# Attention and FP4 feed-forward on one core: two periods as one pattern, later due times, and a last block by tiles on VectorE

## The chip, the core and the metric

The kernel runs on one core of a Trainium2 chip. Times are device microseconds of one execution; the kernel before took 3674.7 us (median of 3 runs, 3671.81 to 3677.18). A profile is one further execution. Engines in its rows: PE is TensorE's matmuls, PEld its weight loads, DVE is VectorE, ACT ScalarE, POOL GpSimd, SP the engine that issues most transfers. PSUM is the accumulator memory that TensorE writes; a tile of 128 x 512 f32 fills one of its 8 banks.

## What is computed

One transformer block on x of 4 x 2048 x 256, f32: attention with 16 heads of 16, a layer norm, a gated feed-forward whose inputs and weights are quantized to FP4 in blocks of 16, and a second norm.

```python
q, k, v = (split_heads(x @ W.T) for W in (Wq, Wk, Wv))        # 16 heads of 16
attn = softmax(q @ k.T * 0.25)
x = layernorm(x + merge(attn @ v) @ Wo.T)

def fp4_linear(x, w):       # both through fp4_quant_dequant: per block of 16,
    ...                     # scale = max|x| / 6, x / scale to the nearest of
    ...                     # 0 .5 1 1.5 2 3 4 6, times scale
h = silu(fp4_linear(x, w_gate)) * fp4_linear(x, w_up)         # 704 columns
x = layernorm(x + fp4_linear(h, w_down))
```

## The kernel before

**Steps and periods.** A step is one batch entry, one block of 512 queries (QB) and one group of four heads: 64 steps. Each goes over 16 tiles of 128 keys; one key tile of one step is a *period*, so there are N = 1024. In period n three things happen for the attention. `maxima` (L394) forms scores for the step that is LEAD = 20 periods ahead: two calls (i = 0, 1), each two matmuls `pm`, of the heads j = 0 and 1 of a pair, into one tile of two banks, from which VectorE takes a maximum per row (`mx`, L409). `exponentials` (L435) forms the scores transposed, four matmuls `pe`, each into a bank of its own, and ScalarE takes the exponential of each into an `e` tile (L443). `values` (L446) multiplies the four `e` tiles of LAG = 2 periods ago with v, into the one bank `av`.

The score matmuls use half of the array's 128 rows: head j = 0 lies in rows 0 to 63 (the upper half below), j = 1 in rows 64 to 127 (the lower half). The row maxima are folded into two spare rows of q (`max_rows`, L411), so that the exponential needs no bias. At a step's end `normalize` (L460) copies `av` out, turns it (`pa`), and VectorE divides (`rd`, `oq`); every second step `oq` is turned (`pr`) into `oT`.

**Parts.** All other work of TensorE is cut into parts by generators: projections of q, k and v (`project`: `ptx`, `pq`, `pv`), the weights' preparation (`prepare`), and per query block `feed_forward` (L597): residual `py`, transposes `ptq`, gates `pg` and `pu`, transposes `pth`, and `pz`. A part ends at a `yield` of its cost; costs of LEAST = 300 and more count. `period` (L666) takes one counted part from the urgent queue (`max_rows`, `normalize`) or the queue, at the end of each period, two in the 20 periods before the first exponentials.

**Order.** TensorE runs in program order as written (`keep_in_program_order`, L133). In each period it is pm of i = 0 and 1, pe of i = 0, av, pe of i = 1, then the part. The other engines' orders are made by the framework's scheduler from the dependences. The 8 banks: `ps_m` two tiles of two banks (pm), `ps_av` one, `ps_x` three in turn for every pe and every part. `later` (L116) puts a step on a list by a due period: the quantization (`fp4`, L145) is so split, since its first half goes from VectorE (block maximum `amax`, scale `sc`, reciprocal `rs`) to GpSimd (`xn`), and its second (`rounded`) from VectorE (`m`) to GpSimd (three steps on `xn`, L163 to L165). GpSimd also does residual adds, gate products and the norm.

**Loads.** q, k and v go to DRAM once (`qx`, `kx`, `vx`; v through two tiles `vt`) and are loaded per step: k a quarter at a time in every fourth period, 28 periods ahead of its exponentials and 8 ahead of its maxima, into 20 tiles of `k`.

**The end.** After the last period the queue runs on alone. The last query block, whose feed-forward can begin only then, takes VectorE instead of GpSimd for every second tile.

Of the kernel before, what the change touches and what calls it, by code (L numbers as in the profile page):

```python
# [29 lines left out]
F32 = mybir.dt.float32  # L32
F32R = mybir.dt.float32r
I32 = mybir.dt.int32
# [18 lines left out]
LEAD = 20  # L53
LAG = 2
LEAST = 300.0
PSUM = bass.MemoryType.PSUM
# [17 lines left out]
def block_kernel(  # L74
# [69 lines left out]

    def fp4(pool, t, tag, gain=1.0, engine=None):  # L145

        p, nb, _ = t.shape
        amax = pool.tile([p, nb], F32, tag="amax" + tag, name="amax")
        nc.vector.tensor_reduce(amax, t, AX.X, ALU.max, apply_absolute_value=True)  # L149
        sc = pool.tile([p, nb], F32, tag="sc" + tag, name="sc")  # L150
        nc.vector.tensor_scalar(sc, amax, gain / 6.0, 1e-12, ALU.mult, ALU.max)
        rs = pool.tile([p, nb], F32, tag="rs" + tag, name="rs")
        nc.vector.reciprocal(rs, sc)
        engine = engine or nc.gpsimd
        engine.tensor_scalar(rs, rs, gain * TIES_DOWN, 1.0, ALU.mult, ALU.mult)
        xn = pool.tile([p, nb, FB], F32, tag="xn" + tag, name="xn", bufs=3 if tag else 2)
        engine.tensor_tensor(xn, t, rs.unsqueeze(2).to_broadcast([p, nb, FB]), ALU.mult)

        def rounded():
            m = pool.tile([p, nb, FB], F32, tag="m" + tag, name="m", bufs=1)  # L160
            nc.vector.tensor_single_scalar(m.bitcast(I32), xn.bitcast(I32), EXPONENT, ALU.bitwise_and)
            nc.vector.tensor_scalar(m, m, 1.0, ROUND, ALU.max, ALU.mult)  # L162
            engine.tensor_tensor(xn, xn, m, ALU.add)  # L163
            engine.tensor_tensor(xn, xn, m, ALU.subtract)  # L164
            engine.tensor_tensor(xn, xn, sc.unsqueeze(2).to_broadcast([p, nb, FB]), ALU.mult)  # L165

        return xn, later(1, rounded, 4 if tag == "" else 2)

# [12 lines left out]
    wdT = const.tile([P, NFC, D], F32, tag="wdT", name="wdT")  # L181
    vt = [const.tile([P, NG, QT // 2, NP, 3 * DH], F32, tag=f"vt{i}", name=f"vt{i}") for i in range(2)]
    for t in vt:
# [60 lines left out]
    def prepare():  # L244
# [9 lines left out]
        nc.scalar.copy(woT.rearrange("p k n -> p (k n)"), pt)  # L254
        yield 500

# [36 lines left out]
        for piece, after in zip(pieces, pieces[1:] + [None]):  # L293
            following = load(*after) if after else None
            yield from transposed(*piece, *q)
            q = following
            yield 500

# [13 lines left out]
    def project(b, tb, what):  # L312
# [7 lines left out]
        for kc in range(KC):  # L320
            pt = psum("ptx")
            for t in range(QT):
                transpose(pt[:, t * P : (t + 1) * P], xb[:, t, kc * P : (kc + 1) * P], ident)
            nc.scalar.copy(xT[:, kc, :], pt)
            yield 600
        for name, c in [(w[0], int(w[1])) for w in what if w != "v"]:
            w, dst = (wkT, kx[b % 2][c][:, :, rows]) if name == "k" else (wqT, qx[(b * NQB + tb) % len(qx)][c])
# [16 lines left out]
            projected.add((b, tb, name + str(c)))  # L344
        for t in range(QT if "v" in what else 0):
            v = vt[t // 2]
            pv = psum("pv")
            for kc in range(KC):
                matmul(
                    pv[:, :D], xT[:, kc, t * P : (t + 1) * P], wvT[:, kc, :], start=(kc == 0), stop=(kc == KC - 1)  # L350
                )
            src = pv[:, :D].rearrange("p (g i j d) -> p g i j d", g=NG, i=NP, j=2)
            for j in range(2):
                nc.scalar.copy(v[:, :, t % 2, :, 2 * j * DH : (2 * j + 1) * DH], src[:, :, :, j, :])
            if t % 2:
                t0 = tb * QT + t - 1
                for g in range(NG):
                    nc.sync.dma_start(vx[b % 2][g, :, t0 : t0 + 2, :], v[:, g].rearrange("p t i c -> p t (i c)"))
            if t == QT - 1:
                projected.add((b, tb, "v"))  # L360
            yield 900

# [14 lines left out]
    def load_k(s, kb):  # L377
        b, qb, g = steps[s]
        for i in range(NP):
            c, h = divmod(g * HG + i * 2, NC)  # L380
            k = p1.tile([P, QB], F32R, tag="k", name="k", bufs=20)
            for j in range(2):
                nc.sync.dma_start(
                    k[R * j : R * j + R, :].bitcast(F32), kx[b % 2][c][:, h + j, kb * QB : (kb + 1) * QB]
                )
            k_sb[s, i, kb] = k
# [47 lines left out]

    def exponentials(s, kt, i):  # L435
        kb, col = kt // QT, kt % QT * P
        pe = [psum("pe") for _ in range(2)]
        for j in range(2):
            rows = slice(R * j, R * j + R)
            matmul(pe[j], k_sb[s, i, kb][rows, col : col + P], q_sb[s, i][rows, :], start=True, stop=True)  # L440
        for j in range(2):
            e = p1.tile([P, QB], F32, tag="e", name="e", bufs=10)
            nc.scalar.activation(e, pe[j], AF.Exp, scale=SCALE)  # L443
            e_sb[s, kt, 2 * i + j] = e

# [14 lines left out]
    def normalize(s):  # L460
# [15 lines left out]
        for i in range(NP):  # L476
# [5 lines left out]
            )  # L482
        yield 500
        if s % 2 == 0:
            return
        yield 0
        pr = psum("pr")
# [4 lines left out]
        oTs[s // 2] = oT  # L492
        yield 500

# [18 lines left out]
    def residual(b, qb, x1, xq):  # L513

        for t in range(QT):
# [10 lines left out]
            if t % 2:  # L526
                layer_norm(x1, t - 1, 2)
                tiles = x1[:, t - 1 : t + 1].rearrange("p t (b f) -> p (t b) f", f=FB)
                later(3, lambda tiles=tiles: xq.append(fp4(p2, tiles, "")))
            yield 900  # L530

    def gated(xqT, h, t, engine):
        for half in range(2):
# [14 lines left out]
            nc.scalar.activation(a, pg[:, :FH], AF.Tanh, scale=0.5)  # L548
            engine.tensor_mul(a, a, g)  # L549
            engine.tensor_add(a, a, g)  # L550
            yield 1200
# [10 lines left out]
            nc.scalar.copy(u, pu[:, :FH])  # L562
            engine.tensor_mul(h[:, cols], a, u)  # L563
            yield 1200

    def turned(hq, tiles, hT):
# [4 lines left out]
        for t in range(2):  # L571
# [3 lines left out]
            nc.scalar.copy(hT[:, t, :4, :].rearrange("p c n -> p (c n)"), pt)  # L575
            yield 500
        pt = psum("pth").rearrange("p (t c n) -> p t c n", t=2, c=2)
# [4 lines left out]
        for c in range(4, NFC):  # L582
            w = min(P, FF - c * P)
            nc.scalar.copy(hT[:w, :, c, :], pt[:w, :, c - 4, :])
        yield 500

# [10 lines left out]
    def feed_forward(b, qb, between):  # L597
        rows = slice(qb * QB, (qb + 1) * QB)
        last = b == B - 1 and qb == NQB - 1
        x1 = p1.tile([P, QT, D], F32, tag="x1", name="x1", bufs=2)  # L600
# [11 lines left out]
        for kc in range(KC):  # L612
# [4 lines left out]
            nc.scalar.copy(xqT[:, kc, :], pt)  # L617
            yield 500
        hq = {}

        def gate(t):

            engine = nc.vector if last and t % 2 else nc.gpsimd
            h = p2.tile([P, FF], F32, tag="h", name="h")
            yield from gated(xqT, h, t, engine)
            blocks = h.rearrange("p (b f) -> p b f", f=FB)
            later(1, lambda: hq.update({t: fp4(p2, blocks, "h", gain=0.5, engine=engine)}))

        def out_rows(t):
            layer_norm(x1, t, 2)  # L630
            at = slice(qb * QB + t * P, qb * QB + (t + 2) * P)
            nc.sync.dma_start(out[b, at, :].rearrange("(t p) d -> p t d", p=P), x1[:, t : t + 2, :])

# [17 lines left out]
        out_rows(2)  # L651


    queue, urgent = deque(), deque()
# [10 lines left out]

    def period(parts):  # L666

        take_due()
        for _ in range(len(urgent)):
# [5 lines left out]
        while parts > 0 and queue:  # L675
            parts -= (part(queue) or 0.0) >= LEAST

# [28 lines left out]

    for n in range(-LEAD, N + LAG):
        m = n + LEAD
        (sm, im), (s, kt), (sv, kv) = divmod(m, NKT), divmod(n, NKT), divmod(n - LAG, NKT)
        if m in (8, 10, 12, 14):  # L710
# [17 lines left out]

        for i in range(NP):
            if m < N:  # L730
                maxima(sm, im, i)
        for i in range(NP):
            if 0 <= n < N:
                exponentials(s, kt, i)
            if i == 0 and n >= LAG:
                values(sv, kv)
        if m < N and im == NKT - 1:
            urgent.append(max_rows(sm))
        if n >= LAG and kv == NKT - 1:
            urgent.append(normalize(sv))  # L740
            if sv % NG == NG - 1:
                queue.append(chain(*steps[sv][:2]))
        period(1 if n >= 0 else 2)
    banks["more"] = True
    while urgent or queue or due:
        period(1)

# [32 lines left out]
```

## Time and profile before

| what | where it is read | value |
|---|---|---|
| median of the runs | times | 3674.7 us |
| the profiled execution, its own time | times | 3676.19 us |
| its span, first to last instruction | page | 3674.4 us |
| first av, and first pm of period 20 | timeline | 106.17, 97.3 us |
| last pm; end of attention | timeline | 3516.7, 3581.2 us |
| mx: reductions on VectorE | groups | 2048 of 1217 ns, 2409.1 us |
| e: exponentials on ScalarE | groups | 4096 of 596 ns, 2217.9 us |
| transfers, mean | page | 89 GB/s |

The page gives busy time per engine, the chain of work that ended last, and the costliest groups. A period's length is read from the timeline as the distance between two first pm matmuls. By the kind of part that stands in a period, the trace has these means over all of the loop: pg 3.78 us (120 periods), pu 3.78 (120), pq 3.54 (110), pv 3.39 (48), py 3.43 (60), pth 3.06 (73), pa 3.07 (59), pn 3.05 (48), and 2.73 where there is none (104, the median 2.61). TensorE's clock was granted in full from 300 to 3581 us but for 3.4 us, 0.91 to 0.92 before and 0.75 after.

### The profile page before, as it was taken

The page shows a single profiled execution, that of the slowest core. Times are in us where ns is not written, and L with a number is a line of the kernel's source. Part 1 is how long each engine was busy: PE and PEld are TensorE (multiplying, and loading weights), DVE is VectorE, ACT ScalarE, POOL GpSimd, SP SyncE. Part 2 cuts the span into 40 slices and gives each one's busy share as a digit, 9 for nine tenths or more (in the row PEclk, how much of TensorE's full clock was granted, in tenths as well). Part 3 has the DMA queues.
Part 4 walks back from the last instruction along what each step waited for, and adds up shares of the span by engine and source line. Part 5 has one row for each costly group of instructions (what it writes and reads, how often), then busy time and mean ns, then how long its engine had stood idle before and what let it go on. Part 6 is the DMA issues. An engine that isn't in the chain of part 4 may idle for free.

```text
span 3674.4 us, 57830 instructions
## 1 busy us (share of the span) xinstructions
PE 3535.7 (96%) x21396; PEld 1598.0 (43%) x21396; DVE 2805.1 (76%) x3250; ACT 2692.1 (73%) x5452; POOL 1292.8 (35%) x1542
## 2 busy tenths in 40 slices
PE   7889999999999999999999999999999999999995
PEld 4333444444444444444444444444443434444343
DVE  4777878777787878778787787877778788878824
ACT  3667777777777777777777777777777777777772
POOL 1340423424243242424324253343424325241525
PEclk9999999999999999999999999999999999999997
DMA  6543323323232322323233232332322222222100
GB/s 207 176 128 100 106 75 106 99 75 111 80 95 91 106 82 84 115 68 115 84 91 100 85 101 79 100 92 70 115 79 59 75 81 59 73 68 87 47 7 6
DMA packets 192146, 328.41 MB, mean 89 GB/s; under 512 B 25848, under 2 KB 69752, under 8 KB 191864
## 3 DMA queue, kind: packets, MB, share of 16 engines
q1 hardware_dynamic: 190472, 323.39, 28.7%
q8 instruction: 171, 2.80, 0.3%
q10 hardware_dynamic: 1392, 1.31, 0.1%
q14 instruction: 111, 0.91, 0.1%
HBM read 237.04 MB, written 86.51 MB: 88 GB/s over the span
## 4 chain that ended last, share of the span: by engine, by line
PE 82%; DVE 12%; POOL 3%; DMA 2%; ACT 1%; issue 1%; SPq 0%; POOLq 0%; ACTq 0%; DVEq 0%
PE av L134 24%; PE pe L134 18%; PE pm L134 15%; DVE mx L409 8%; PE pz L134 6%; PE pg L134 5%; PE pu L134 5%; PE pq L134 3%; PE pv L134 2%; PE pth L137 1%; DMA q<-qx 1%; PE pa L137 1%; PE py L134 1%; PE pn L137 1%; DVE amax L149 1%; DVE st L501 1%
## 5 line engine op out<-in xcount | busy, mean ns | idle before, releaser
L409 DVE TENSOR_REDUCE mx<-pm 128x2 f32<-128x1024 f32 x2048 | 2409.1, 1217 | 670.2 <-PE pm L134 665.7
L443 ACT ACTIVATE e<-pe 128x512 f32<-128x512 f32 x4096 | 2217.9, 596 | 678.4 <-PE pe L134 672.7
L134 PE MATMUL av<-e,v 128*32 128x512 f32 x8192 | 1097.1, 607 | 1.4 <-DMA v<-vx 1.4
L134 PE MATMUL pe<-q,k 64*128 64x512 f32 x4096 | 1035.4, 456 | 5.0 <-ACT e L443 4.7
L134 PEld LDWEIGHTS pe<-q,k 64*128 64x128 f32 x4096 | 475.1, 184 | 967.3 <-ACT e L443 853.4
L134 PE MATMUL pm<-k,q 62*128 62x512 f32 x4096 | 804.4, 448 | 69.2 <-DVE mx L409 59.6
L134 PEld LDWEIGHTS pm<-k,q 62*128 62x128 f32 x4096 | 346.5, 185 | 384.2 <-DVE mx L409 177.4
L134 PEld LDWEIGHTS av<-e,v 128*32 128x32 f32 x8192 | 162.1, 108 | 333.1 <-issue 313.2
L549 POOL TENSOR_TENSOR a<-a,g 128x352 f32<-128x352 f32 x124 | 116.1, 936 | 499.6 <-ACT a L548 499.6
L594 POOL TENSOR_TENSOR x<-x,read 128x128 f32<-128x128 f32 x128 | 59.0, 461 | 494.2 <-ACT read L142 494.2
L134 PE MATMUL pz<-wdT,hT 128*128 128x128 f32 (+1 forms) x1536 | 231.2, 293 | 0.0
L163 POOL TENSOR_TENSOR xn<-xn,m 128x704 f32<-128x704 f32 (+2 forms) x104 | 159.6, 1534 | 154.6 <-DVE m L162 136.0
L134 PEld LDWEIGHTS pz<-wdT,hT 128*128 128x128 f32 (+1 forms) x1536 | 191.9, 191 | 45.8 <-ACT e L443 18.2
L563 POOL TENSOR_TENSOR h<-a,u 128x352 f32<-128x352 f32 x124 | 116.1, 937 | 227.0 <-ACT u L562 224.6
L525 POOL TENSOR_TENSOR x<-x,read 128x256 f32<-128x256 f32 x64 | 46.7, 730 | 400.4 <-ACT read L142 400.2
L134 PE MATMUL pg<-wgT,xqT 128*128 128x352 f32 x512 | 187.0, 488 | 0.0
L134 PE MATMUL pu<-wuT,xqT 128*128 128x352 f32 x512 | 185.2, 484 | 0.0
L164 POOL TENSOR_TENSOR xn<-xn,m 128x704 f32<-128x704 f32 (+2 forms) x104 | 159.9, 1538 | 5.7
L165 POOL TENSOR_TENSOR xn<-xn,sc 128x704 f32<-128x704 f32 (+2 forms) x104 | 131.5, 1264 | 7.8
L550 POOL TENSOR_TENSOR a<-a,g 128x352 f32<-128x352 f32 x124 | 118.9, 958 | 9.7
L134 PEld LDWEIGHTS pg<-wgT,xqT 128*128 128x128 f32 x512 | 88.2, 191 | 58.4 <-ACT e L443 19.2
L134 PEld LDWEIGHTS pu<-wuT,xqT 128*128 128x128 f32 x512 | 87.7, 189 | 58.4 <-ACT e L443 20.0
(95 smaller groups left out, 2277.3 us busy)
## 6 DMA issues: line engine op xcount, KB each, us to landing
k<-kx SPq DMA_DIRECT2D x1024, 128.0 KB
v<-vx SPq DMA_DIRECT2D x64, 768.0 KB
q<-qx SPq DMA_DIRECT2D x256, 124.0 KB
kx<-khi SPq DMA_DIRECT2D x64, 256.0 KB
qx<-qhi SPq DMA_DIRECT2D x64, 256.0 KB
vx<-vt SPq DMA_DIRECT2D x128, 96.0 KB
xb<-in_L_attn_x_dram SPq DMA_DIRECT2D x16, 512.0 KB
kx<-klo SPq DMA_DIRECT2D x32, 256.0 KB
```

The source lines that it names most:

```text
L134: tc.keep_in_program_order(nc.tensor.matmul(*args, **kw))
L137: tc.keep_in_program_order(nc.tensor.transpose(*args))
L163: engine.tensor_tensor(xn, xn, m, ALU.add)
L164: engine.tensor_tensor(xn, xn, m, ALU.subtract)
L165: engine.tensor_tensor(xn, xn, sc.unsqueeze(2).to_broadcast([p, nb, FB]), ALU.mult)
L409: nc.vector.tensor_reduce(mx_sb[s][:, t, 2 * i : 2 * i + 2, kb], pm, AX.X, ALU.max)
L443: nc.scalar.activation(e, pe[j], AF.Exp, scale=SCALE)
L525: nc.gpsimd.tensor_add(x1[:, t, :], x1[:, t, :], read(py[:, :D]))
L549: engine.tensor_mul(a, a, g)
L550: engine.tensor_add(a, a, g)
L563: engine.tensor_mul(h[:, cols], a, u)
L594: nc.gpsimd.tensor_add(x1[:, t, cols], x1[:, t, cols], read(pz))
```

## The change

Two periods become one pattern, given by a string. In it m and n are the two `maxima` of the even and the odd period, e and f the four exponentials of each, one by one, v and w the values; q takes two parts in a row, r what q left over. `more` replaces `period`; a part whose cost is TIED ends a row of two early. `max_rows` and `normalize` are begun at once and no longer at the end of the period.

```diff
+ORDER = "m0 e0 m1 e1 q e2 n0 e3 v n1 f0 f1 r f2 w f3".split()
+TIED = 500.0
+E_BUFS = 12
...
-    def exponentials(s, kt, i):
+    def exponentials(s, kt, h):
+        i, j = divmod(h, 2)
         kb, col = kt // QT, kt % QT * P
-        pe = [psum("pe") for _ in range(2)]
-        for j in range(2):
-            rows = slice(R * j, R * j + R)
-            matmul(pe[j], k_sb[s, i, kb][rows, col : col + P], q_sb[s, i][rows, :], start=True, stop=True)
...
+        pe = psum("pe")
+        rows = slice(R * j, R * j + R)
+        matmul(pe, k_sb[s, i, kb][rows, col : col + P], q_sb[s, i][rows, :], start=True, stop=True)
+        e = p1.tile([P, QB], F32, tag="e", name="e", bufs=E_BUFS)
...
         while parts > 0 and queue:
-            parts -= (part(queue) or 0.0) >= LEAST
+            cost = part(queue) or 0.0
+            parts -= cost >= LEAST
+            if cost == TIED:
+                break
+        return parts
...
-    for n in range(-LEAD, N + LAG):
+    for n in range(-LEAD, N + LAG, 2):
+        left = 0
+        if n == N - NKT:
+            x1_last = load_last(*steps[-1][:2])
+        for step in ORDER:
+            n_of = n + (step[0] in "nfwr")
+            m = n_of + LEAD
+            if step in ("m0", "n0"):
+                loads(n_of)
+                take_due()
+            if step[0] in "mn" and m < N:
+                maxima(*divmod(m, NKT), int(step[1]))
+                if step == "n1" and (m + 1) % NKT == 0:
+                    begin(max_rows(m // NKT))
+            elif step[0] in "ef" and 0 <= n < N:
+                exponentials(*divmod(n_of, NKT), int(step[1]))
+            elif step in "vw" and n >= LAG:
+                s, kt = divmod(n_of - LAG, NKT)
+                values(s, kt)
+                if kt == NKT - 1:
+                    begin(normalize(s))
+                    if s % NG == NG - 1 and s + 1 < len(steps):
+                        queue.append(chain(*steps[s][:2]))
+            elif step == "q":
+                left = more(2)
+            elif step == "r" and n < 0:
+                more(2)
+            elif step == "r":
+                while left > 0 and queue:
+                    left -= (part(queue) or 0.0) >= LEAST
...
+    feed_forward_last(*steps[-1][:2], x1_last)
```

Buffers, the v transfers and the due times:

```diff
-            k = p1.tile([P, QB], F32R, tag="k", name="k", bufs=20)
+            k = p1.tile([P, QB], F32R, tag="k", name="k", bufs=16)
...
+                v = vt[(tb * 2 + t // 2) % 3]
...
-                for g in range(NG):
-                    nc.sync.dma_start(vx[b % 2][g, :, t0 : t0 + 2, :], v[:, g].rearrange("p t i c -> p t (i c)"))
+                    nc.sync.dma_start(
+                        vx[b % 2][:, :, t0 : t0 + 2, :].rearrange("g p t c -> p g (t c)"),
+                        v.rearrange("p g t i c -> p g (t i c)"),
+                    )
...
-        return xn, later(1, rounded, 4 if tag == "" else 2)
+        return xn, later(2, rounded, 4 if tag == "" else 2)
...
-                layer_norm(x1, t - 1, 2)
-                tiles = x1[:, t - 1 : t + 1].rearrange("p t (b f) -> p (t b) f", f=FB)
-                later(3, lambda tiles=tiles: xq.append(fp4(p2, tiles, "")))
+                def normed(t=t):
+                    layer_norm(x1, t - 1, 2)
+                    tiles = x1[:, t - 1 : t + 1].rearrange("p t (b f) -> p (t b) f", f=FB)
+                    later(4, lambda: xq.append(fp4(p2, tiles, "")))
+                later(2, normed)
...
-            later(1, lambda: hq.update({t: fp4(p2, blocks, "h", gain=0.5, engine=engine)}))
+            later(3, lambda: hq.update({t: fp4(p2, blocks, "h", gain=0.5)}))
```

The last query block has functions of its own, which go tile by tile. In them VectorE does what GpSimd did, but for two small steps of the norm (`rstd`); `fp4_at_once` is the whole of `fp4` on VectorE.

```diff
+        def moments(t):
+            st = p2.tile([P, 6], F32, tag="st", name="st")
+            nc.vector.bn_stats(st, x1[:, t, :])
...
+            nc.gpsimd.tensor_scalar_add(rstd[:, :1], mv[:, 0, 1:2], LN_EPS)
+            nc.gpsimd.tensor_tensor(rstd[:, :1], rstd[:, :1], minus_half[:, :1], ALU.pow)
...
+        def attended(t):
...
+            nc.vector.tensor_add(x1[:, t, :], x1[:, t, :], py[:, :D])
+            moments(t)
+        def quantized(t):
+            normed(t)
+            xq[t] = fp4_at_once(p2, x1[:, t].rearrange("p (b f) -> p b f", f=FB), "")
...
+        def hidden(t):
+            h = p2.tile([P, FF], F32, tag="h", name="h")
+            for half, (a, g, u) in enumerate(gates.pop(t)):
+                nc.vector.scalar_tensor_tensor(a, a, 1.0, g, ALU.add, ALU.mult)
+                nc.vector.tensor_mul(h[:, half * FH : (half + 1) * FH], a, u)
+            hq[t] = fp4_at_once(p2, h.rearrange("p (b f) -> p b f", f=FB), "h", gain=0.5)
...
+        attended(0)
+        attended(1)
+        quantized(0)
+        up(0)
+        attended(2)
+        quantized(1)
+        up(1)
+        hidden(0)
+        attended(3)
+        quantized(2)
+        pz = downward(0)
+        up(2)
+        hidden(1)
+        added(0, pz)
+        quantized(3)
+        pz = downward(1)
+        up(3)
+        hidden(2)
+        stored(0)
+        added(1, pz)
+        pz = downward(2)
+        hidden(3)
+        stored(1)
+        added(2, pz)
+        pz = downward(3)
+        stored(2)
+        added(3, pz)
+        stored(3)
```

Here `up` is a tile's transposes and its pg and pu, `downward` its pth and pz, `stored` the norm's last step and the store.

## The prediction

> **What bounds the kernel now.** I read the page's engine shares and chain of waits first, then the windows by stage, the timeline of TensorE inside two periods, the waits between 300 and 3540 us, and last the groups by form for prices.
>
> ```profile
> PE 3535.7 (96%) x21396; PEld 1598.0 (43%) x21396; DVE 2805.1 (76%) x3250; ACT 2692.1 (73%) x5452; POOL 1292.8 (35%) x1542
> PE 82%; DVE 12%; POOL 3%; DMA 2%; ACT 1%; issue 1%; SPq 0%; POOLq 0%; ACTq 0%; DVEq 0%
> ...
> 300.00:3516.70 3216.70, 3177.84 (x19481) 1413.26 (x19479) 2564.98 (x2941) 2455.60 (x4931) 1144.74 (x1356) 1.00 0.28 86
> 3516.70:3581.20 64.50, 60.16 (x375) 25.35 (x371) 7.08 (x19) 48.31 (x99) 14.27 (x23) 1.00 0.03 9
> 3581.20:3674.40 93.20, 49.42 (x216) 36.23 (x216) 40.11 (x71) 19.65 (x48) 52.97 (x64) 0.75 0.02 6
> ```
>
> TensorE is the path for 3,480 us; the last 93 us belong to GpSimd and VectorE by turns. Inside the loop, two neighbouring periods:
>
> ```profile
> 2012.09 0.73 PE L134 MATMUL pm<-k,q 62*128 62x512 f32 x4
> 2012.66 0.57 PE L134 MATMUL pe<-q,k 64*128 64x512 f32 x2
> 2013.16 1.07 PE L134 MATMUL av<-e,v 128*32 128x512 f32 x8
> 2014.16 0.50 PE L134 MATMUL pe<-q,k 64*128 64x512 f32 x2
> 2014.59 0.66 PE L137 MATMUL pth<-ident,xn 128*128 128x128 f32 x4
> 2015.17 0.73 PE L134 MATMUL pm<-k,q 62*128 62x512 f32 x4
> 2015.74 0.58 PE L134 MATMUL pe<-q,k 64*128 64x512 f32 x2
> 2016.26 1.06 PE L134 MATMUL av<-e,v 128*32 128x512 f32 x8
> 2017.25 0.49 PE L134 MATMUL pe<-q,k 64*128 64x512 f32 x2
> 2017.68 1.45 PE L134 MATMUL pg<-wgT,xqT 128*128 128x352 f32 x4
> 2019.06 0.50 PE L134 MATMUL pm<-k,q 62*128 62x512 f32 x2
> ```
>
> Read the starts. The period with pg takes 3.89 us, of which 0.19 is a wait of pe for its bank; the shortest such period of the trace is 3.70. Its pieces: pm 0.57, pe 0.33, av 1.00, pe 0.43, pg 1.38. A pair of score matmuls on the two row halves of the array costs one "unit": within pm it is 0.231 us (timeline at 2015.51 to 2015.74). Each stretch of score matmuls carries about 0.195 more, being 0.10 ahead of its second unit and 0.10 at its end, and a part carries 0.20 (pg: four passes of 0.295 make 1.18 of the 1.38). So a period with a part costs TensorE 2.32 + 0.20 + W, W being the part's passes: pg 1.18, pq, pv and py 0.86, pz 1.32, four transposes 0.40. The medians of the trace bear this out (pg 3.72, pq 3.39). From period 80 on, 942 periods took 3187.5 us, where these sums give 3044: 143 us are waits.
>
> ```profile
> PEld pe L134 <- ACT e L443: 786.7, 1029, 1.3
> ...
> PEld pm L134 <- DVE mx L409: 144.8, 363, 1.2
> ```
>
> The first line is mostly weight loads ready early; it costs only the 0.18 us of short periods (pth, 3.10 instead of 2.92). The second is the real wait, a VectorE that has not emptied pm.
>
> **The skill.** "TensorEngine Tiling (Array Packing)", Key Properties, says that a change of tiling mode drains the array and that tiles run independently; the 0.2 us per change and the paired starts agree. "TensorE: Matmul & The Clock Gate", Part 3, The mechanism, says that matmuls themselves keep strict program order. This trace differs:
>
> ```profile
> 1172.14 0.50 PE L134 MATMUL pm<-k,q 62*128 62x512 f32 x1
> 1172.35 0.27 PE L134 MATMUL pz<-wdT,hT 64*128 64x128 f32 x1
> 1172.38 0.47 PE L134 MATMUL pm<-k,q 62*128 62x512 f32 x1
> ```
>
> In the program both pz passes (upper rows) stand before both pm; yet a pm starts 0.2 us ahead of the second pz. I take it for the lower half passing what waits for the upper. "Perfetto Trace Analysis", Optimization Strategy, says that consistent bubbles can mean that PSUM has no room for the next tile; pth's 0.18 us agrees.
>
> **The change part by part.**
>
> (1) TensorE's order. Per two periods, score stretches fall from four to three, part stretches from two to one. That is -0.195 - 0.20 = -0.40 us. But the score matmuls no longer go in pairs. Counting each row half as its own stream: f3 m0 e0 m1 e1 is 4 units (lower half f3, m0, m1, e1), e2 n0 e3 is 2, n1 f0 f1 f2 is 3. Nine units for eight: +0.23. Sum: 9 x 0.231 + 3 x 0.195 + 2.0 for av = 4.67, +0.20 + W = 4.87 + W, against 5.03 + W before; -0.16. Without a part the first two stretches join: 6 + 3 units, 4.47. From the order of TensorE's instructions, the 501 double periods with both kinds of scores hold 736 us of W; 36 have no part. Base: 465 x 4.87 + 36 x 4.47 + 736 = 3162 us, for what took 3418.8 us (97.3 to 3516.2).
>
> (2) The waits that come back, walked through with durations of the trace (pe to activation 0.43, or 0.53 at a stretch's start; exponential 0.49 apart, 0.60 long; reduction 1.18; release to load 0.05 to 0.17).
> - The first part takes f3's bank: free at 0.53 + 0.60 + 0.05 = 1.18, wanted at 1.12. 465 x 0.06 = 28.
> - No part: n0 needs m0's buffer, free at 0.77 + 1.18 + 0.17 = 2.12; the double then lasts 5.67, 1.2 over its base. 36 x 1.2 = 43. Before, such periods took 2.61 each.
> - pa keeps its bank until VectorE, behind m0 and m1 (to 3.13), has done rd and oq (0.75). With a second part e3 wants it: 4.05 against 3.0 to 3.3; 38 x 0.84 = 32. Alone (23 times, oq behind n0): 1.6 each, 37. Before, pa cost no wait (mean 3.07).
> - Nine single pn or pr: 4. VectorE's other steps, 396 us in all (2805.1 - 2409.1), meet short doubles in about a hundred cases: 30 as an estimate, 0 to 100.
> - Weight preparation before period 80: some 45 of today's 54 stay.
> Sum 3162 + 219 = 3381, so -38. The large e pool, 16 instead of 20 k buffers and the later due times cost nothing while a load has eight periods (about 26 us) to land; SyncE now waits for the last exponentials of period n-1 before it issues k, and behind it stand q, v and the kx writes, which are wanted later still.
>
> (3) Start: a third vt and one vx transfer for four. ScalarE's 19.7 us of waits on vx shrink; TensorE's share of that was 4.4 us at 75.97 and four smaller ones. -8.
>
> (4) Periods without maxima: 22, now 2.93 each; the long stretches spread the exponentials, -3.
>
> (5) The last block. Today GpSimd's quantization and VectorE's share one chain:
>
> ```profile
> L164 POOL TENSOR_TENSOR xn<-xn,m 128x704 f32<-128x704 f32 x64 | 109.0, 1703 | 2.6
> L164 DVE TENSOR_TENSOR xn<-xn,m 128x704 f32<-128x704 f32 x2 | 1.8, 875 | 0.0
> ```
>
> On VectorE alone a tile costs: residual add 0.42, moments 0.59, norm 0.25, quantize 256 columns 3.0, gates 4 x 0.5, quantize 704 columns 6.3, and 0.42 + 0.59 + 0.25 at the end: 13.8, four tiles 55, some 3 less as neighbours overlap. Ahead of it stands what stands there now, 4.3 us to the first add; behind the last quantization come transposes, copies, pz, norm and store, 9 us, of which 2.6 lie under the sum. 4.3 + 52 + 4 of waits + 9 = 69, against 93.2. -24. A GpSimd that works alongside made VectorE's add 1.26 us instead of 0.88; here GpSimd has only rstd. Bounds: -30 with no waits, -10 if each tile waits 4 us for TensorE.
>
> Sum: 3674.4 - 38 - 8 - 3 - 24 = 3601 us of span; the profiled run reports 3676.2 for a span of 3674.4, and the median is 3674.7, so 3602.
>
> **The rivals.**
> A, slower: matmuls keep strict order across the halves, as the skill says. e2 n0 e3 is then 3 units, 10 in all: 465 x 0.231 = +107, 3709. It decides from 0.15 us per double on (73 / 501). Against it speaks 1172.14, for it that this is one pattern of few matmuls.
> B: the waits of VectorE's in-order queue eat the loop's gain: 70 us instead of 30, and pa more. Only start and end remain: 3640 to 3680. For it: VectorE is 76% busy and 5.5 of a double's 6.7 us.
> C: the waits in (2) hardly occur, since the chains run half a period apart: 120 us less, 3500 to 3530. For it, 143 us of waits now sit at pm, which the new order separates by whole stretches.
> That the change doesn't do what it says: the instruction order shows the alternation in all 501 doubles; only the r slot is almost never filled.
>
> **Numbers.** Main case 3565 to 3640: 0.58. A 0.15. B 0.17, of which 0.05 within 0.2% and 0.01 slower. C 0.10. A measurement here tells 0.2% (7 us) from no change. Faster 0.79, same 0.05, slower 0.16. The range 3530 to 3690 leaves out A and half of C.
>
> **What would show it.** Right: three score stretches of about 1.1, 0.66 and 0.9 us per double, n0 starting beside e2 and not after it; big doubles (pg with pu) of 7.2 to 7.4 us against 7.55; empty ones near 5.7; pa doubles long; a tail of about 70 us. Wrong: e2 n0 e3 of 0.9 us; VectorE's lag showing as waits of pm in long doubles; a tail over 85 us; or a lower granted clock in the loop, now 1.00.

## The result and the profile after

The changed kernel takes 3798.1 us (median of six runs, 3794.6 to 3799.7) against 3674.8 for the kernel before, run beside it: a ratio of 1.033, interval 1.032 to 1.035. The forecast was 3602, so even its sign was wrong. The profiled execution has a span of 3793.1 us, against 3674.4.

The engine shares and the chain of waits from the page of the changed kernel, then its windows by stage (columns: busy us and instructions of PE, PEld, DVE, ACT and POOL, granted clock, transfers):

```profile
PE 3587.7 (95%) x21348; PEld 1653.3 (44%) x21348; DVE 2821.5 (74%) x3310; ACT 2648.3 (70%) x5446; POOL 1259.7 (33%) x1495
PE 70%; DVE 16%; POOL 6%; ACT 4%; issue 3%; DMA 1%; SPq 0%; POOLq 0%; ACTq 0%; DVEq 0%
```

```profile
300.00:3646.10 3346.10, 3216.22 (x19403) 1462.12 (x19403) 2559.20 (x2928) 2407.96 (x4912) 1152.08 (x1353) 0.99 0.28 83
3646.10:3716.90 70.80, 67.48 (x406) 30.41 (x402) 8.13 (x21) 50.88 (x105) 19.86 (x29) 1.00 0.02 7
3716.90:3793.10 76.20, 49.56 (x168) 31.77 (x168) 50.64 (x131) 16.24 (x42) 8.52 (x16) 0.85 0.03 9
```

Read the chain first: TensorE's share fell from 82% to 70%, and VectorE and GpSimd together rose from 15% to 22%. The rows of the windows then say where: the long one (the loop) is 129 us longer than before, the last (the tail) 17 us shorter. TensorE was idle for 129.9 us of the loop's window; before it was 38.9. By stage, with the loop counted from the first pm of period 20 to the last pm:

| stage, us | before | forecast | after |
|---|---|---|---|
| start, to the first pm of period 20 | 97.3 | 89 | 92.8 |
| loop | 3419.4 | 3381 | 3553.4 |
| periods without maxima | 63.8 | 61 | 69.9 |
| tail, from the last av | 93.9 | 70 | 77.0 |

The waits of VectorE between 300 and 3500 us (us in total, times, longest) show what is new. Before:

```profile
DVE mx L409 <- PE pm L134: 605.2, 578, 2.3
DVE rd L472 <- PE pa L137: 13.5, 30, 0.6
DVE m L161 <- POOL xn L157: 5.1, 26, 0.2
DVE st L501 <- POOL x L525: 3.4, 15, 0.2
```

After:

```profile
DVE mx L443 <- PE pe L140: 396.8, 440, 3.9
DVE st L533 <- POOL x L630: 121.6, 56, 2.9
DVE mx L443 <- PE pm L140: 109.1, 241, 1.8
DVE amax L155 <- POOL x L541: 56.3, 28, 2.5
DVE amax L155 <- POOL h L599: 42.4, 39, 1.4
DVE m L166 <- POOL xn L162: 18.5, 25, 0.7
DVE st L533 <- POOL x L557: 6.9, 14, 0.5
```

A VectorE that waits for TensorE (mx) is only ahead of it, and that costs nothing. A VectorE that waits for GpSimd holds up everything behind in its queue, also the reductions that TensorE needs. Those waits were 8.5 us and are 245.7. TensorE's waits for them, in the same stretch of the changed kernel:

```profile
PE pm L140 <- DVE mx L443: 96.1, 127, 4.4
...
PEld pm L140 <- DVE mx L443: 274.5, 288, 4.7
...
PEld pm L140 <- DVE st L533: 44.3, 52, 1.5
```

Before, the first two were 37.6 and 144.8, and the third was 5.0. One such place, as the timelines of VectorE, GpSimd and TensorE show it (start, length, what; in brackets the idle time before and its releaser):

```profile
1508.58 0.41 DVE L533 BATCH_NORM_STATS2 st<-x 128x6 f32<-128x256 f32 x1
...
1512.92 0.69 DVE L155 TENSOR_REDUCE amax<-x 128x32 f32<-128x512 f32 x1 [1.87 <-POOL x L541]
1513.52 0.63 DVE L451 TENSOR_TENSOR nh<-nm,nh 128x16 fp32r<-128x16 f32 x1
1514.07 3.48 DVE L443 TENSOR_REDUCE mx<-pm 128x2 f32<-128x1024 f32 x3
```

```profile
1510.98 0.70 POOL L537 TENSOR_TENSOR rstd<-rstd,minus_half 128x2 f32<-128x2 f32 x1
1511.79 1.09 POOL L541 TENSOR_SCALAR x<-x,minus,rstd 128x256 f32<-128x256 f32 x2
```

```profile
1511.93 0.49 PE L140 MATMUL pe<-q,k 64*128 64x512 f32 x1
1515.34 0.79 PE L140 MATMUL pm<-k,q 62*128 62x512 f32 x2 [2.92 <-DVE mx L443]
```

VectorE's moments (st) of a tile and its block maximum (amax) of the normed tile, with GpSimd's norm between them, stand so close together in VectorE's queue that amax must wait 1.87 us for the norm to end at 1512.9. Behind it and one short step (nh) stand the reductions of the two pm that are full, and there are only two such tiles: TensorE waits 2.92 us for the first. (The third reduction of the row is that of the pm which TensorE writes at 1515.34.) The same wait of 2.9 us comes back in ten query blocks between 598 and 2661 us: the ten double periods with eight ptx there took 12.1 us on average, against 6.5 in the first run below. The wait has a second price, in the windows around it:

```profile
1507.10:1513.80 6.70, 5.15 (x33) 2.35 (x29) 4.83 (x14) 4.83 (x9) 4.59 (x8) 1.00 0.33 88
1513.80:1520.60 6.80, 5.26 (x20) 1.73 (x24) 5.12 (x7) 1.58 (x4) 2.63 (x3) 0.50 0.20 68
```

The granted clock (the column before the last two) is halved for 6.8 us. Added up over 300 to 3500 us, TensorE ran at half clock for 92.2 us; before it was 3.4.

### The profile page after: what moved, and what is told of

It is laid out like the page before. It is cut to its first block, busy times and chain, and to the rows that moved or that the text cites. A ratio compares the mean times of both kernels' runs of the same rounds, so it can differ in the third digit from the quotient of the medians.

```text
span 3793.1 us, 57775 instructions
## 1 busy us (share of the span) xinstructions
PE 3587.7 (95%) x21348; PEld 1653.3 (44%) x21348; DVE 2821.5 (74%) x3310; ACT 2648.3 (70%) x5446; POOL 1259.7 (33%) x1495
## 4 chain that ended last, share of the span: by engine, by line
PE 70%; DVE 16%; POOL 6%; ACT 4%; issue 3%; DMA 1%; SPq 0%; POOLq 0%; ACTq 0%; DVEq 0%
PE av L140 20%; PE pe L140 16%; PE pm L140 12%; DVE mx L443 10%; PE pz L140 5%; PE pg L140 4%; PE pu L140 4%; PE pq L140 2%; ACT e L476 2%; PE pth L143 1%; DVE amax L155 1%; PE pv L140 1%; POOL h L599 1%; PE pn L143 1%; POOL xn L162 1%
## 5 line engine op out<-in xcount | busy, mean ns | idle before, releaser
L443 DVE TENSOR_REDUCE mx<-pm 128x2 f32<-128x1024 f32 x2048 | 2434.2, 1217 | 575.9 <-PE pe L140 433.9
L476 ACT ACTIVATE e<-pe 128x512 f32<-128x512 f32 x4096 | 2195.0, 602 | 640.8 <-PE pe L140 598.1
L140 PE MATMUL pe<-q,k 64*128 64x512 f32 x4096 | 1321.1, 427 | 12.9 <-DVE oq L510 9.9
L140 PE MATMUL pm<-k,q 62*128 62x512 f32 x4096 | 1137.8, 460 | 134.2 <-DVE mx L443 124.8
L140 PEld LDWEIGHTS pe<-q,k 64*128 64x128 f32 x4096 | 617.4, 188 | 674.6 <-ACT e L476 485.8
L140 PEld LDWEIGHTS pm<-k,q 62*128 62x128 f32 x4096 | 487.4, 187 | 676.5 <-DVE mx L443 338.5
L585 POOL TENSOR_TENSOR a<-a,g 128x352 f32<-128x352 f32 x120 | 112.3, 936 | 594.9 <-ACT a L584 594.9
L140 PEld LDWEIGHTS pz<-wdT,hT 128*128 128x128 f32 x1488 | 189.1, 192 | 53.1 <-ACT e L476 24.0
L533 DVE BATCH_NORM_STATS2 st<-x 128x6 f32<-128x256 f32 x120 | 50.8, 423 | 169.5 <-POOL x L630 162.1
L148 ACT COPY read<-pz 128x128 f32<-128x128 f32 x120 | 31.8, 265 | 143.1 <-PE pm L140 91.1
```

Of the source, the lines that this page charges most:

```text
L140: tc.keep_in_program_order(nc.tensor.matmul(*args, **kw))
L443: nc.vector.tensor_reduce(mx_sb[s][:, t, 2 * i : 2 * i + 2, kb], pm, AX.X, ALU.max)
L476: nc.scalar.activation(e, pe, AF.Exp, scale=SCALE)
L533: nc.vector.bn_stats(st, r[:, t0 + t, :])
L585: nc.gpsimd.tensor_mul(a, a, g)
```

## The experiments

Theory Q: VectorE's order is made by the framework's scheduler, which places a step where its own reckoning has the inputs ready. With the new pattern it puts st, amax and m ahead of reductions at places where GpSimd is not done. (The traces show the order that came out; how the scheduler reckons is an assumption.) Rivals: the later due times themselves put the steps there (D); TensorE's new pattern is slow by itself (the forecast's A and B, P in the expectations); the halved clock is the cause and not the consequence (C in the expectations, another one than the forecast's).

**VectorE in the program's order.** All of VectorE's instructions of the changed kernel are held in program order:

```diff
+    class InOrder:
+        def __getattr__(self, name):
+            return lambda *args, **kw: tc.keep_in_program_order(getattr(nc.vector, name)(*args, **kw))
+    vec = InOrder()
...
-        nc.vector.tensor_reduce(mx_sb[s][:, t, 2 * i : 2 * i + 2, kb], pm, AX.X, ALU.max)
+        vec.tensor_reduce(mx_sb[s][:, t, 2 * i : 2 * i + 2, kb], pm, AX.X, ALU.max)
```

> The changed kernel with every VectorE instruction pinned to program order, so that a step put on the list for a later period stands in VectorE's queue where the program puts it. Theory Q (VectorE's queue waits for GpSimd: st, amax and m were placed ahead of reductions whose data was ready): VectorE's waits for GpSimd between 300 and 3640 us, 252 us in the changed kernel, fall under 60, TensorE's waits for pm fall by some 150, and the time is 3600 to 3690. Theory P (the pattern itself is slow: nine units instead of eight, and two pm buffers that the double period turns over too rarely): 3760 to 3810, with waits for GpSimd gone or not. Theory C (the clock, halved once in each query block, is the cause and not the consequence): over 3750, the halvings stay.

Measured: 3674.0 us, ratio to before 1.000 (0.999 to 1.001). VectorE's waits of the loop now (the steps that are held in order have the helper's line, L142):

```profile
DVE mx L142 <- PE pe L147: 479.6, 517, 2.5
DVE mx L142 <- PE pm L147: 113.2, 335, 1.7
DVE st L142 <- issue: 0.2, 1, 0.2
```

No wait for GpSimd is left, and the loop is 3428.0 us, 125.4 less than after. So the instructions and the due times do little harm when they run in the order in which they are written; the order that the scheduler made does. Counted in the traces, st, amax and m stand on average 5 to 8 reductions earlier in the changed kernel's VectorE queue than in this run's, and four reductions are a double period. One thing is not held apart: GpSimd's order, also the scheduler's, came out otherwise too (at least 276 of its 1495 instructions stand in another place; ScalarE's order is the same), so the 125 us are the price of both orders together. Half clock fell to 41.0 us, so 92.2 - 41.0 of it belongs to the stalls; at half clock at most half of the time is lost, 26 of the 125 us, so C falls. The loop is still 9 us longer than before: the pattern's gain is missing, and these 9 us are all that is left for P; the section on the reasons takes this up.

**VectorE in order in the loop alone.** The same, but the last block's instructions are left to the scheduler.

> VectorE pinned to program order in the loop alone, the last block free as in the changed kernel. Theory Q: the loop of the first run of this kind (3424 us from period 20 to 1022), the tail of the changed kernel (76 instead of 85 us): 3660 to 3670. Theory P: the same; this run parts tail from loop.

Measured: 3666.2 us, 0.998 (0.997 to 0.999). With the free order the tail is 78.7 us, with the fixed one it was 85.2. The fixed order is not free either: in the last block it took 6.5 us.

**GpSimd's data replaced by constants.**

```diff
-        nc.vector.tensor_reduce(amax, t, AX.X, ALU.max, apply_absolute_value=True)
+        nc.vector.tensor_reduce(amax, same if still else t, AX.X, ALU.max, apply_absolute_value=True)
...
-            nc.vector.bn_stats(st, r[:, t0 + t, :])
+            nc.vector.bn_stats(st, wkT[:, 0, :])
```

> The changed kernel in which VectorE's block maxima, exponents and norm statistics in the loop read a constant tile instead of what GpSimd has written: the quantization's scales and the norms' moments are left out as functions of the data, all instructions stay. VectorE then never waits for GpSimd in the loop. Theory Q: 3580 to 3680, no waits for GpSimd at st, amax or m, and the clock halvings in the loop vanish with the stalls. Theory P: above 3750. Theory C: above 3720 with the halvings still there.

Measured: 4187.1 us, a single run; a miss.

```profile
DVE m L169 <- POOL xn L172: 231.4, 75, 4.6
...
DVE mv L537 <- POOL minus L542: 57.9, 49, 2.3
DVE sc L159 <- POOL xn L173: 16.6, 13, 1.3
```

With their inputs always there the steps were placed earlier still (st by 154 reductions on average against the changed kernel), and then waited for the buffers that they write, which GpSimd had still to read. To take a dependence away from a step that a scheduler places moves the step too, so this run does not price the wait. It shows that 306 us of such waits on buffers do the same harm: half clock rose to 406 us.

**The old order, all else as changed.**

```diff
-ORDER = "m0 e0 m1 e1 q e2 n0 e3 v n1 f0 f1 r f2 w f3".split()
+ORDER = "m0 m1 e0 e1 v e2 e3 q n0 n1 f0 f1 w f2 f3 r".split()
...
-                left = more(2)
+                more(1 if n >= 0 else 2)
...
-                while left > 0 and queue:
-                    left -= (part(queue) or 0.0) >= LEAST
+                more(1)
```

> The changed kernel with the order of before inside the double period (both maxima, two exponentials, values, two exponentials, one part, then the same again), due times, buffers, v transfers and last block as changed. Theory Q: the due times don't hold VectorE's steps back, so little waits for GpSimd as in the kernel before (some 10 to 40 us), and the tail and start save 20: 3640 to 3670. If the later due times are the cause and not the pattern: 3740 to 3800. Theory P: 3640 to 3670 as well.

Measured: 3653.4 us (3651.1 to 3653.9), 0.994 (0.993 to 0.996). VectorE waits 18.1 us for GpSimd. The fastest kernel of the study: start (92.5), tail (75.7) and due times stay, the loop is 3415.6, against 3419.4 before.

**The kernel before with only the new last block.**

> The kernel before with the changed last block alone. All theories: the loop as before, the tail 76 instead of 93 us as in the changed kernel: 3650 to 3665.

Measured: 3657.0 us, 0.995 (0.994 to 0.996); tail 78.5 us against 93.9. So of the 22 us that the run with the old order gains, 18 are the last block's.

**The due times of before in the changed kernel.**

```diff
-        return xn, later(2, rounded, 4 if tag == "" else 2)
+        return xn, later(1, rounded, 4 if tag == "" else 2)
...
-                    later(4, lambda: xq.append(fp4(p2, tiles, "")))
-                later(2, normed)
+                    later(3, lambda: xq.append(fp4(p2, tiles, "")))
+                normed()
...
-            later(3, lambda: hq.update({t: fp4(p2, blocks, "h", gain=0.5)}))
+            later(1, lambda: hq.update({t: fp4(p2, blocks, "h", gain=0.5)}))
```

> The changed kernel with the due times of before (norms at once, quantization after 3, 1 and 1 periods). Theory Q (what stalls VectorE is where the scheduler puts its steps in the new pattern, and it puts them where its own reckoning has the data ready, whatever the due period): waits of VectorE for GpSimd in the loop 200 to 320 us as in the changed kernel (252), time 3770 to 3830. Theory D (the later due times themselves push the steps to bad places): waits under 80 us, time 3660 to 3720.

(In `out_rows` the norm is likewise done at once.) Measured: 3787.6 us, a single run, loop 3551.1. The waits of VectorE for GpSimd are 161 us instead of 245.7, and the loop is the same, though some parts also stand at other places in TensorE's order: D falls. It also shows that the sum of these waits is no measure of the loss: which of them TensorE feels depends on what stands behind.

**The old order with two parts in a row, free and in order.** The string is the old one as above, the two lines with `more` stay as changed. In the second run the loop's VectorE is also held in order.

> The changed kernel with the order of before for scores and values, but with both parts of a double period in a row after the first period's second exponentials, and none in the second. By TensorE's sums: 8 units, three score stretches and one part stretch, 4.63 + W per double instead of 5.03 + W. If TensorE's sum decides: the loop falls by 100 to 160, time 3500 to 3560. If the wait for banks comes back where four exponentials and both maxima now stand in one stretch (0.4 us per double) and parts that were alone in a period no longer hide it: 3630 to 3680. Theory Q adds a loss if VectorE's steps are put ahead of reductions again: then waits for GpSimd over 100 us and over 3680.

> The kernel of the run before last on the old order with both parts in a row (3926 us), with VectorE's instructions of the loop held in the program's order. If its 270 us over the old order with single parts are the scheduler putting VectorE's steps ahead of GpSimd's data, this run comes to 3640 to 3690 us with no wait of VectorE for GpSimd left. If two parts in a row cost by themselves in the old order (banks of ScalarE late, maxima in a row late), it stays above 3750 us without such waits.

Measured: free 3926.6 us, 1.068 (1.067 to 1.070); in order 3773.6, a single run. The fixed order takes 207 us of waits for GpSimd away and 153 us of time. The 110 us that are left over the old order with single parts and VectorE in order (3663.7, below) are another thing. Waits of TensorE in the run in order, 300 to 3500 us:

```profile
PE pm L147 <- DVE mx L142: 151.7, 424, 1.2
...
PEld pm L147 <- DVE mx L142: 371.5, 558, 1.5
```

In the old order with single parts, also held in order (the last run below), these are 50.0 and 142.1. With both parts at one place, m0 and m1 of one period and n0 and n1 of the next come close together and find their buffers still in VectorE's hands. So the alternation is what makes two parts in a row bearable.

**The new order with single parts, free and in order.** (In the first 20 periods three parts stand in a double instead of four.)

```diff
             elif step == "q":
-                left = more(2)
-            elif step == "r" and n < 0:
-                more(2)
+                more(1 if n >= 0 else 2)
             elif step == "r":
-                while left > 0 and queue:
-                    left -= (part(queue) or 0.0) >= LEAST
+                more(1)
```

> The changed kernel with its new order of scores and values, but one part at each of the two places of the queue as before. If the two parts in a row bring on VectorE's early steps, the waits of VectorE for GpSimd fall from 252 us to under 60 and the time to 3640 to 3700 us. If the new order of scores and values brings them on by itself, they stay above 150 us and the time above 3740 us.

> The new order of scores and values with one part at each of the two places of the queue (3942 us when the scheduler orders VectorE), with VectorE's instructions of the loop held in the program's order. If all of the loss there is VectorE waiting for GpSimd ahead of reductions, it comes to 3660 to 3700 us like the changed kernel in order. If the new order needs both parts in a row because TensorE's extra part stretch and its bank waits cost by themselves (about 0.6 us in 460 double periods, 270 us at most), it stays above 3750 us without such waits.

Measured: free 3942.4 us, 1.073 (1.071 to 1.074), with 231.5 us of VectorE waiting for GpSimd, so the new order of scores and values brings the early steps on by itself. In order 3801.7 us, a single run, with no such wait left: both theories of that run hold a part, 141 us for VectorE's order, 135 us for TensorE's own time against the new order with parts in a row. The windows of the run in order:

```profile
300.00:3500.00 3200.00, 3149.53 (x18504) 1381.62 (x18496) 2453.31 (x2780) 2294.43 (x4687) 1100.28 (x1298) 1.00 0.28 84
```

TensorE is idle for only 50 us of these 3200; it does 18504 matmuls in the time, where the changed kernel in order did 19249 in the same stretch. The doubles themselves are longer: eight pth take at least 6.53 us, against 5.95 with both parts in a row, four pa 6.53 against 5.59. By the string, the score matmuls need a stretch more and some matmuls of one half no longer have a partner on the other; the trace gives the sum, not the split.

**The old order with VectorE held in order,** the control for the first run.

> Order of before, later due times, VectorE pinned in the loop: the control for the pin. If the pin is neutral where VectorE did not wait for GpSimd (theory Q): 3645 to 3670. If the pin is a gain of itself, whatever the pattern: under 3620. If it costs: over 3680.

Measured: 3663.7 us, a single run; loop 3429.8 against 3415.6. The fixed order costs 14 us of loop where nothing was to be gained; the executions of the two kernels in order that ran ten times and more spread over 9 and 12 us, so one run does not fix this size. All together (us; waits of VectorE for GpSimd from 300 to 3500):

| scores and values | parts | VectorE's order | time | waits |
|---|---|---|---|---|
| old | single | scheduler's | 3653.4 | 18 |
| old | single | program's (loop) | 3663.7 | 0 |
| old | in a row | scheduler's | 3926.6 | 207 |
| old | in a row | program's (loop) | 3773.6 | 0 |
| new | single | scheduler's | 3942.4 | 232 |
| new | single | program's (loop) | 3801.7 | 0 |
| new | in a row (the change) | scheduler's | 3798.1 | 246 |
| new | in a row | program's (loop) | 3666.2 | 0 |

Two things can be read off. The scheduler's order costs 132 to 153 us in three of the four patterns, and gains 10 in the old one (by one run). There too st, amax and m stand 3 to 6 reductions earlier than in program order, but VectorE waits only 18 us for GpSimd; why this suffices in the old pattern and not in the others is not shown. And in program order each half of the new pattern costs 110 and 138 us over the old one, while the two together come level with it and no further.

## Why the prediction was wrong

**The step that failed** is the one in (2) that reads "VectorE's other steps, 396 us in all (2805.1 - 2409.1), meet short doubles in about a hundred cases: 30 as an estimate, 0 to 100". It counted VectorE's other steps by how long they are, and not by how long they wait for GpSimd with reductions behind them. Program order takes 125.4 us off the loop; that much of the loss the runs show to be the scheduler's order, which made 245.7 us of waits for GpSimd where the program's order has none. Since the fixed order may have a price of its own (14 us of loop in the old pattern, by one run), the harm may be that much more. The forecast said of "the later due times" that they cost nothing. Of the loads beside which that sentence stood it is right (no wait for a transfer is among those of the changed kernel from 300 to 3500 us), and the due times turned out not to be the cause; but the forecast has no term for where VectorE's steps land in its queue. It took TensorE's order from the changed kernel and not VectorE's, although that is the one which nobody writes by hand.

**(1), TensorE's pattern, was right.** The timeline of the changed kernel has the three score stretches, and n0 beside e2:

```profile
2003.23 0.50 PE L140 MATMUL pe<-q,k 64*128 64x512 f32 x1
2003.23 0.73 PE L140 MATMUL pm<-k,q 62*128 62x512 f32 x2
...
2005.50 0.50 PE L140 MATMUL pe<-q,k 64*128 64x512 f32 x1
2005.51 0.73 PE L140 MATMUL pm<-k,q 62*128 62x512 f32 x2
2005.87 0.50 PE L140 MATMUL pe<-q,k 64*128 64x512 f32 x1
```

In the program the order is e2, n0, e3, and n0's matmul on the lower half starts with e2 (2005.51 and 2005.50). In the single records its own partner on the upper half comes 0.34 us later, at 2005.84. This is rival A refuted, and with it the strict order that "TensorE: Matmul & The Clock Gate", Part 3, The mechanism, states, as the forecast had taken from the kernel before. The shortest double with pg and pu takes 7.29 us, the sum said 7.23 + 0.06. Doubles with two pz take 7.99 where the sum gives 7.51: each pz ends with two passes over half the rows, which before ran beside the next pm; behind the first pz of a row the second follows instead, and the starts around those passes are 0.20 us apart, not 0.11 (1170.79 to 1171.41 us of the run in order). 42 such doubles make 20 us that were missed.

**(2), the waits that come back,** seen in the run with VectorE in order, whose loop of 3428.0 is 47 us over the forecast. Doubles without a part: 5.59 at the least (forecast 5.67), but 6.73 on average, 81 us over their base where 43 were forecast. Where VectorE is busy for at most 5.5 us of such a double, it lasts 5.6 to 5.7; where more of its other steps falls in, it is busy for 6.2 to 7.7, and the double lasts 6.3 to 10.1. pa went the other way: alone 5.87 instead of 6.87, with a second part 0.55 instead of 0.84 over; together some 34 us less than forecast. 38 + 20 - 34 leaves 23 of the 47 unassigned; the half clock of 41.0 us, unforeseen, can be at most 20 of them. TensorE's waits for reductions in that run:

```profile
PE pm L147 <- DVE mx L142: 37.3, 57, 2.0
...
PEld pm L147 <- DVE mx L142: 191.6, 254, 2.3
```

The second stands at 144.8 before. This fits rival B: less work for TensorE per double would make VectorE's queue the limit more often. No run tests it apart.

**(3) and (5), start and tail, were right in kind.** The start gained 4.5 of 8 us. The tail gained 16.9 of 24. VectorE's busy time in it, 50.6 us, is the 52 of the sum; its waits between the first add and the last quantization are 11.1 us instead of 4: the longest, 2.95, is for ScalarE's gates (g) of the first tile, where no other tile is far enough to fill in. **(4)** was wrong by sign: 6 us longer instead of 3 shorter. With the old due times it is 63.3, as before. So in this pattern the later due times bring these 6 us; in the old order, which keeps them, the stretch is 65.2, and why it is so much less there is open.

**The rivals.** The forecast's one slower rival was about TensorE, busy for 96% of the span. What decided was a wait for GpSimd, busy for 35%. B named the right queue, and gave its cost an upper end at which the loop's gain is merely gone (a slower kernel had 0.01 of its 0.17); the measured loop is 134 us longer than before. The forecast's C, that the waits hardly occur, falls too: even in order the loop is 47 us over the main case and not 120 under it. Of the signs of being wrong, waits of pm in long doubles (2.92 us in one of 12.0) and "a lower granted clock in the loop" came true.

## What to carry to other kernels

When a change moves the instructions of an engine whose order a scheduler makes, read that engine's new order too, and ask of every step that waits for a third engine what stands behind it. If steps wait for a slower engine in the middle of a queue that feeds the bound engine, holding that queue in program order is a quick test of whether the order is to blame; it moves other engines' orders too, and has a price of its own, here 6.5 us in the last block and, by one run, 10 us of time in the old pattern. Parts of a pattern don't add up: in program order each half of this one cost over 100 us alone, and both together nothing.

## What the runs showed of the hardware

The clock fell to half during a single wait of 2.92 us, and stayed there for 6.8 us; in that stretch groups of four av matmuls start 0.85 us apart (1516.49 and 1517.34), just before it 0.45 (1508.26 and 1508.71). "TensorE: Matmul & The Clock Gate", Part 1, gives about 3.4 us of idleness for this; here the halved stretch begins at 1513.8, 1.4 us after TensorE's last matmul before the wait ended (1511.93 + 0.49). So a wait shorter than that length can set it off, but it need not. From 300 to 3500 us, 15 of the changed kernel's 17 waits of 1.4 us and more had a half-clock stretch begin in them or soon after; with the loop alone in order it was 8 of 22 waits of 1.1 to 2.0 us. From 600 to 2880 us the changed kernel pays this once in 229 us, which belongs to the price of a stall: in the stretch shown TensorE works for 5.26 of the 6.8 us, so at most 2.6 us of work are lost.
